# A graph layer's gather and sum: a product with zeros ahead of each product, and more chunks gathered by ScalarE

## The chip, the cores and the metric

The kernel runs on 1 core of one Trainium2 chip. The metric is the device time of one execution in microseconds (us); less is better. TensorE (PE), VectorE (DVE), ScalarE (ACT), GpSimd (POOL) and SyncE (SP) each work through their own instructions in a fixed order and wait for each other by semaphores.

## The reference, cut to what matters

```python
# x: (12500, 128) f32; src, dst: (200000,) int32, sorted by dst
h = jnp.maximum(_layernorm(x, axis=-1), 0.0)
agg = jax.ops.segment_sum(h[src], dst, num_segments=12500)
deg = jax.ops.segment_sum(jnp.ones(200000), dst, num_segments=12500)
agg = agg / jnp.maximum(deg, 1.0)[:, None]
y = jax.nn.relu(agg @ Wg + h @ Ws + bg)     # 128 -> 128
y = jnp.tanh(y @ W1 + b1)                   # 128 -> 512
y = jnp.tanh(y @ W2 + b2)                   # 512 -> 512
return x + (y @ W3 + b3)                    # 512 -> 128
```

For each of 200000 edges a row of 128 numbers is fetched and added to the row of the edge's target; the means go through a small network.

## The kernel before

**Tiling.** The edges are cut into 1563 chunks of 128, in the order of their targets. The 12500 nodes are cut into blocks of 512 columns (smaller ones at the end). As targets are sorted, a chunk's targets lie in a window of 24 columns whose place is loaded into a PE register (`place`).

**The sum.** For a chunk, `rows` holds the 128 fetched rows and `oh` a 0/1 matrix of 128 by 24 that VectorE makes by comparison (`onehot`, L495), for 8 chunks at a time. `add(c)` (L643) multiplies them on PE and adds the product into the block's sum `acc[b]` in PSUM, or into `edge[b]`, a PSUM tile of up to 280 columns for chunks that may reach into two blocks. Such a tile is first written with zeros by `cleared`. All PE work is kept in program order by the class `pe` (its line is L378 for matmuls, L381 for transposes), and in f32 a matmul is two weight loads and two matmul records in the trace.

**Four ways to fetch rows.** The layer-normed nodes lie in DRAM (`htab`) and, turned, in SBUF (`tab`, 128 features by 12544 nodes).

- `gather` (L386): one indirect DMA by POOL for a chunk, into one of `AHEAD` = 24 buffers. 1323 chunks go this way, in the list `order`, and a buffer is free again when `add` has used it.
- `row_loads` (lane 0): 128 DMAs by SyncE, one row of 512 bytes each, at an address from a register; 4 buffers.
- `column_copies` (lane 1): 128 copies by ScalarE, each of one column of `tab` at an address from a register (L442); 16 addresses are loaded at a time.
- `column_pairs` (lane 2): 64 instructions by VectorE, each of which puts two columns together (L451); 16 addresses are loaded at a time.

Chunks of the last two ways are columns, not rows: `turn` (L456) transposes them on PE into a `pm` tile and ScalarE copies them out as `turned` (L476). 80 more chunks, spread in 10 groups of 8, are fetched as raw rows of `x` at the start and normed on the way.

`SHARES` (L48) says how many chunks go to lanes 0, 1 and 2; the slots are every fourth chunk between 104 and 1540, dealt out evenly. `load_times` spreads the copies and loads of a lane over the chunks between its uses, in steps of four copies, four rows or eight pairs, so that they are issued between the other work of their engine.

**The network.** The layers of a block (`part0` to `part4`) are cut into single PE products of up to 512 columns, and one of them is put between the products of the chunks at every second chunk; ScalarE brings each result out of PSUM through its activation (`h`, L473), and the next product needs it. Three `pm` tiles are shared by these products, the turned chunks and the degree counts. From chunk 1312 on (`QUICK`) a small planner with costs per product decides how many network steps go ahead of each chunk.

**The start.** About 200 us are spent on layer norm, indices and weights; the sums begin in between, and the copies of lanes 1 and 2 after some 240 us.

Of the kernel before, what the change touches and what calls it, by code (L numbers as in the profile page):

```python
# [22 lines left out]
F32 = mybir.dt.float32  # L23
# [8 lines left out]
P = 128  # L32
# [12 lines left out]
SPREAD = 8  # L45
EVERY = 4
AT = 3
SHARES = 14, 50, 96  # L48
FROM, UNTIL = 104, 1540
SBUFS = 4  # L50
MARGIN = 18
# [14 lines left out]
PAST = 255  # L66
MAY_BE_OFF = 240
SEEN = 656
TOLD = 14
EARLY = 3  # L70

# [6 lines left out]
def windowed(ctx, tc, x, src, dst, Wg, Ws, bg, W1, b1, W2, b2, W3, b3, out, flag):  # L78
    nc = tc.nc
# [19 lines left out]
    def raw(c):  # L99
        return RAW0 <= c < RAW1 and (c - RAW0) % STEP < GRP  # L100
# [7 lines left out]
    def window(c):  # L108
        if raw(c):
            return per * (c - c % GRP) + first(W_RAW, per * GRP), W_RAW  # L110
        w = [w for c0, w in WINDOWS if c0 <= c][-1]
        return per * c + first(w), w
# [4 lines left out]
    ahead_of = P + MAY_BE_OFF  # L117
    past_end = P * (each + 1) + SEEN
    pad_dst = 2 * N // (PAST + 1) * (PAST + 1) + PAST
    assert each * N == E and pad_dst >= 2 * N - PAST and 0 < NT * P - N < P  # L120
    under, over = off + -(-ahead_of // each), off + -(-(SEEN - MAY_BE_OFF) // each)
    assert off + max(under, over) <= PAST
# [3 lines left out]
    slots = [c for c in range(AT, NCH, EVERY) if FROM <= c < UNTIL and not raw(c)]  # L126
    owed = [0.5 * n for n in SHARES] + [0.5 * (len(slots) - sum(SHARES))]
    for c in slots:
        owed = [o + n for o, n in zip(owed, [*SHARES, len(slots) - sum(SHARES)])]
        kind = max(range(4), key=lambda k: owed[k])  # L130
# [14 lines left out]
    const = ctx.enter_context(tc.tile_pool(name="const", bufs=1))  # L145
# [30 lines left out]
    for g in range(NRAW):  # L176
        t = raws.tile([P, GRP, D], F32, name=f"raw{g}")
# [7 lines left out]
    ident = const.tile([P, P], F32, name="ident")  # L185
# [27 lines left out]
    bases = const.tile([NROW, CPR], I32, name="bases")  # L213
    zeros = const.tile([P, P], BF16, name="zeros")
    nc.vector.memset(zeros, 0.0)
    begins = const.tile([1, NT], I32, name="begins")
    parity = const.tile([P, 2], F32, name="parity")
    for i in range(2):
# [153 lines left out]
    rows_t, ohs, acc = {}, {}, {}  # L372
# [10 lines left out]
    def sp_dma(*a):  # L383
        tc.keep_in_program_order(nc.sync.dma_start(*a))
# [132 lines left out]
    def seen(t):  # L517

        if t % TOLD == 0:
            u = min(t + TOLD, NT)  # L520
            loads, vs = nc.values_load_multi_w_load_instructions(
# [5 lines left out]
            told.update(enumerate(vs, t))  # L527
        w = ed.tile([P, SEEN], U8, name="nearby", bufs=4)
        at_v = bytes_at[bass.ds(told.pop(t), (P - 1) * each + SEEN)]
        sp_dma(w, bass.AP(tensor=at_v.tensor, offset=at_v.offset, ap=[[each, P], [1, SEEN]]))  # L530
        nearby[t] = w
# [48 lines left out]
    for c in range(NCH):  # L580
        lo, w = window(c)
# [21 lines left out]
    edge = {}  # L603

    def edge_span(b):
        spans = [window(c) for c in across[b]]
        return min(lo for lo, _ in spans), max(lo + w for lo, w in spans)
# [3 lines left out]
    def place(c, a0, a1):  # L611

        if raw(c):
            lo, w = window(c)
            return slice(max(lo, a0), min(lo + w, a1)), slice(max(lo, a0) - lo, min(lo + w, a1) - lo)
        if c not in places_of:
            r, q = divmod(c, CPR)
            k = next((i for i in range(q, CPR) if raw(r * CPR + i) or r * CPR + i == NCH), CPR)
            loads, vs = nc.values_load_multi_w_load_instructions(
                bases[r : r + 1, q:k], engines=[mybir.EngineType.PE], min_val=0, max_val=N - W,  # L620
                skip_runtime_bounds_check_because="brought between its ends on VectorE",
            )
            for ld in loads:
                tc.keep_in_program_order(ld)
            places_of.update(enumerate(vs, c))
        lo, w = window(c)
        most = min(lo + w, a1) - W
        at_v = places_of.pop(c).with_bounds(min_val=min(max(lo, a0), most), max_val=most)
        return bass.ds(at_v, W), slice(0, W)

    def moved(s, by):
        if isinstance(s, slice):
            return slice(s.start - by, s.stop - by)
        return bass.ds(s.start - by, W)

    def cleared(pool, name, w):
        t = pool.tile([P, BLK], F32, name=name)
        pe.matmul(
            t[:, :w], zeros, zeros[:, :1].to_broadcast([P, w]), start=True, stop=False, skip_group_check=True
        )  # L640
        return t

    def add(c):  # L643
        rows, oh = rows_t.pop(c), ohs[c // GRP][:, c % GRP]
        b = min(b for b, cs in enumerate(reach) if c in cs)
        n, m = blocks[b]
        if c in across[b]:
            e0, e1 = edge_span(b)
            if c == across[b][0]:
                edge[b] = cleared(ps_b, "edge", e1 - e0)  # L650
            to, of = place(c, e0, e1)
            pe.matmul(
                edge[b][:, moved(to, e0)], rows, oh[:, of], start=False, stop=(c == across[b][-1]), skip_group_check=True
            )
            if c == across[b][-1]:
                sums = ed.tile([P, 288], F32, name="sums", bufs=4)
                act.copy(sums[:, : e1 - e0], edge.pop(b)[:, : e1 - e0])
                edges[b] = sums
            return
        if b not in acc:  # L660
            acc[b] = cleared(ps_a, "agg", m)
        to, of = place(c, n, n + m)
        pe.matmul(
            acc[b][:, moved(to, n)], rows, oh[:, of], start=False, stop=(c == inside[b][-1]), skip_group_check=True
        )
# [216 lines left out]
    for c in range(NCH):  # L882
# [33 lines left out]
        if c >= QUICK:  # L916
# [4 lines left out]
            while soonest() and max(now, soonest()[2]) < there:  # L921
                go_on(soonest())
            now = max(now, there) + 0.27
        add(c)

        lead = LEAD if c < QUICK else 2
# [359 lines left out]
@with_exitstack  # L1286
def gnn_kernel(ctx: ExitStack, tc: tile.TileContext, *args):
    nc = tc.nc
    keep = ctx.enter_context(tc.tile_pool(name="flags", bufs=1))
    flag = keep.tile([1, 1], I32, name="flag")  # L1290
    with ExitStack() as inner:
        windowed(inner, tc, *args, flag)
    outside = nc.values_load(flag, min_val=0, max_val=P)
    with tc.If(outside > 0):
        with ExitStack() as inner:
            general(inner, tc, *args)
# [31 lines left out]
```

## Time and profile before

| | |
|---|---|
| median of 3 runs | 2167.27 us (2161.28 to 2171.19) |
| the profiled execution | 2164.96 us |
| its span, first to last instruction | 2163.2 us |
| mean granted PE clock | 0.750 |
| busy: PE, DVE, ACT, POOL | 1474.7, 1274.1, 933.4, 1335.4 us |
| gathers by POOL | 1323 of 951 ns |
| column copies by ScalarE | 6400 |
| column pairs by VectorE | 6144 |
| row loads by SyncE | 1792 |

Times are of one profiled execution. An engine's busy time does not count register loads, semaphores or the issue of DMAs. "Issue" as a cause of idle time means that the profile shows nothing the engine waited for; "remote" that the releaser could not be named. In rows of the order of time the columns are the start, the time taken, engine, line, operation, tile written and read, count, and in brackets the idle time before.

### The profile page before, as it was taken

To read this page: it belongs to the slowest core of one execution; us is meant where nothing else is said; L and a number is where in the kernel's file an instruction comes from. 1 tells how busy PE (TensorE), PEld (TensorE's weight loads), DVE (VectorE), ACT (ScalarE), POOL (GpSimd) and SP (SyncE) were. 2 spreads that over 40 slices of the span, in tenths; PEclk is the share of its full clock that TensorE was granted. 3 is DMA by queue.
4 is the path that set the end of the run, shared out by engine and by line. 5 is a ranking of instruction groups with operands and counts; after the bars stand their busy time and mean duration, and the time that the engine had idled before them with its cause. 6 is when DMAs were issued, how large, how long until landed. Compare 5 with 4: busy or idle time off the path is not lost.

```text
span 2163.2 us, 34925 instructions
## 1 busy us (share of the span) xinstructions
PE 1474.7 (68%) x5402; PEld 981.4 (45%) x5402; DVE 1274.1 (59%) x7014; ACT 933.4 (43%) x6907; POOL 1335.4 (62%) x1411
## 2 busy tenths in 40 slices
PE   0025543768687787776885876767787687798587
PEld 0024433445454454454553544545454454454457
DVE  3854365756466675665673765666576476566530
ACT  1201144545544444454544445445454454545432
POOL 7756666566666666666666566666666666666661
PEclk9999985766866766776676776777766776788589
DMA  5934221222221222222222122122222122221210
GB/s 137 243 99 124 58 51 49 52 54 58 54 58 49 61 59 55 54 61 59 52 59 57 49 59 58 51 59 60 51 57 63 47 61 66 53 61 53 56 48 22
DMA packets 132962, 139.16 MB, mean 64 GB/s; under 512 B 31655, under 2 KB 109347, under 8 KB 132536
## 3 DMA queue, kind: packets, MB, share of 16 engines
q0 software_dynamic: 44896, 92.04, 16.7%
q1 hardware_dynamic: 84558, 41.29, 7.1%
q10 hardware_dynamic: 3276, 3.51, 0.6%
q14 instruction: 181, 1.48, 0.2%
q8 instruction: 51, 0.84, 0.2%
HBM read 123.71 MB, written 13.03 MB: 63 GB/s over the span
## 4 chain that ended last, share of the span: by engine, by line
PE 37%; DVE 20%; issue 17%; another core or an unknown queue 11%; ACT 9%; DVEq 2%; DMA 1%; ACTq 1%; SPq 0%
PE pm L378 24%; DVE cols L451 12%; PE agg L378 7%; ACT cols L442 7%; PE edge L378 3%; DVEq L399 2%; ACT h L473 2%; PE pt L381 1%; DVE nearby L535 1%; ACTq L399 1%; PE pm L381 1%; DVE mT L689 1%; DVE oh L495 1%; DVE h L241 1%
## 5 line engine op out<-in xcount | busy, mean ns | idle before, releaser
L388 POOL DMA_INDIRECT rows<-htab,scol x1323 | 1257.7, 951 | 759.7 <-issue 294.0
L451 DVE SCALAR_TENSOR_TENSOR cols<-first_only,tab 128x2 f32<-128x2 f32 x6144 | 913.8, 217 | 404.8 <-issue 394.7
L378 PE MATMUL pm<-h,w 128*128 128x512 f32 (+4 forms) x1344 | 836.1, 724 | 184.1 <-ACT h L473 66.8
L442 ACT COPY cols<-tab 128x1 f32 x6400 | 713.9, 188 | 489.1 <-issue 482.3
L378 PEld LDWEIGHTS agg<-oh,rows 128*128 128x128 f32 x1914 | 420.2, 275 | 285.1 <-issue 269.9
L378 PE MATMUL agg<-oh,rows 128*128 128x24 f32 x1914 | 382.1, 314 | 38.7 <-issue 35.0
L378 PEld LDWEIGHTS pm<-h,w 128*128 128x128 f32 x1344 | 253.7, 237 | 213.7 <-ACT h L473 71.6
L378 PEld LDWEIGHTS edge<-oh,rows 128*128 128x128 f32 x732 | 138.7, 238 | 96.1 <-issue 91.1
L473 ACT ACTIVATE h<-pm,b2c 128x512 f32<-128x512 f32 (+4 forms) x112 | 70.7, 631 | 173.7 <-PE pm L378 57.7
L378 PE MATMUL edge<-oh,rows 128*128 128x24 f32 x732 | 131.3, 286 | 17.6 <-issue 14.0
L805 DVE TENSOR_TENSOR o<-pt,xb 128x512 f32<-128x512 f32 x23 | 15.9, 692 | 203.9 <-remote 83.2
L495 DVE TENSOR_TENSOR oh<-shared,dloc 128x192 f32<-128x192 f32 x186 | 64.8, 350 | 86.2 <-remote 34.1
L473 ACT ACTIVATE h<-pm,b1c 128x512 f32<-128x512 f32 (+4 forms) x112 | 70.1, 631 | 99.5 <-remote 33.6
L476 ACT COPY turned<-pm 128x128 f32<-128x128 f32 x146 | 38.2, 262 | 158.2 <-PE agg L378 60.6
L378 PE MATMUL pm<-ident,cols 128*128 128x128 f32 x192 | 57.9, 394 | 54.8 <-ACT h L473 27.3
L179 POOL DMA_INDIRECT raw<-in_x_dram,rsrc x80 | 76.8, 960 | 25.6 <-issue 24.1
L535 DVE TENSOR_SCALAR_CACHE_REDUCE nearby<-nearby,parity 128x656 uint8<-128x656 uint8 x98 | 87.0, 887 | 6.1 <-issue 6.1
L285 PE MATMUL pm<-ident,idx_f 98*128 98x98 f32 x32 | 6.2, 376 | 108.4 <-DVE idx_f L279 68.5
L378 PEld LDWEIGHTS pm<-ident,cols 128*128 128x128 f32 x192 | 40.9, 257 | 71.3 <-ACT h L473 33.8
L378 PEld LDWEIGHTS agg<-oh,turned 128*128 128x128 f32 x194 | 47.2, 270 | 55.9 <-issue 35.0
L381 PE MATMUL pt<-ident,xb 128*128 128x128 f32 x98 | 27.1, 431 | 61.0 <-issue 32.8
L381 PE MATMUL pm<-ident,degs 128*128 128x128 f32 x99 | 24.9, 374 | 62.9 <-ACT h L473 30.3
(120 smaller groups left out, 808.3 us busy)
## 6 DMA issues: line engine op xcount, KB each, us to landing
srows<-htab SPq DMA_DIRECT2D x1792, 0.5 KB
rows<-htab,scol POOLq DMA_INDIRECT x1323
nearby<-bytes_at SPq DMA_DIRECT2D x98, 82.0 KB
xb<-htab SPq DMA_DIRECT2D x24, 256.0 KB
xb<-in_x_dram SPq DMA_DIRECT2D x23, 256.0 KB
out_dram<-o SPq DMA_DIRECT2D x23, 256.0 KB
xt<-in_x_dram SPq DMA_DIRECT2D x8, 640.0 KB
htab<-h SPq DMA_DIRECT2D x8, 640.0 KB
```

The source lines that it names most:

```text
L179: nc.gpsimd.indirect_dma_start(out=t[:, j, :], out_offset=None, in_=x, in_offset=bass.IndirectOffsetOnAxis(ap=rsrc[:, g, j : j + 1], axis=0),)
L241: nc.vector.scalar_tensor_tensor(h, xt, 0.0, spread(stats[:, 1], k), op0=ALU.max, op1=ALU.mult)
L378: tc.keep_in_program_order(nc.tensor.matmul(*a, **k))
L381: tc.keep_in_program_order(nc.tensor.transpose(*a, **k))
L388: nc.gpsimd.indirect_dma_start(out=r, out_offset=None, in_=htab, in_offset=bass.IndirectOffsetOnAxis(ap=scol[:, c : c + 1], axis=0),)
L399: loads, vs = nc.values_load_multi_w_load_instructions(places[min(lane, 1)][r : r + 1, q // EVERY, p0 : p0 + LOADS[lane]], engines=[kind], ...
L442: tc.keep_in_program_order(nc.scalar.copy(to[:, t : t + 1], of))
L451: last[:] = [tc.keep_in_program_order(nc.vector.scalar_tensor_tensor(to, first_only, a, b.to_broadcast([P, 2]), op0=ALU.mult, op1=ALU.add))]
L473: tc.keep_in_program_order(nc.scalar.activation(*a, **k))
L476: tc.keep_in_program_order(nc.scalar.copy(*a))
L495: newest[:] = [nc.vector.tensor_tensor(oh[:, :k, :w], lane[:, None, :w].to_broadcast([P, k, w]), dloc[:, g * GRP : g * GRP + k][:, :, None ...
L535: done = nc.vector.tensor_scalar(w, w, parity[:, t % 2 : t % 2 + 1], None, op0=ALU.is_equal, op1=ALU.add, accum_out=found[:, t : t + 1])
```

## The change

Three constants change: lane 0 gets 22 chunks, lane 1 gets 90 and lane 2 gets 94, so that 206 chunks are fetched without POOL and 1277 by it. A tile `none` of 96 columns of zeros is set once. Ahead of each chunk's product, `kept_busy` adds a product of the unit matrix with up to 96 columns of zeros to the first columns of the same PSUM tile. It adds nothing to the sums.

```diff
-SHARES = 14, 50, 96
+SHARES = 22, 90, 94
...
+FILL = 96
...
+    none = const.tile([P, FILL], F32, name="none")
+    nc.vector.memset(none, 0.0)
...
+    def kept_busy(t, w):
+
+        w = min(w, FILL)
+        pe.matmul(t[:, :w], ident, none[:, :w], start=False, stop=False, skip_group_check=True)
+
     def add(c):
...
             if c == across[b][0]:
                 edge[b] = cleared(ps_b, "edge", e1 - e0)
+            kept_busy(edge[b], e1 - e0)
             to, of = place(c, e0, e1)
...
         if b not in acc:
             acc[b] = cleared(ps_a, "agg", m)
+        kept_busy(acc[b], m)
         to, of = place(c, n, n + m)
```

## The prediction

> **What bounds the kernel now.** I read the page's head, its chain of work that ended last and its groups, then one table for the long middle stage (400 to 2000 us), the waits in that stage, and single microseconds of the order of time.
>
> ```profile
> span 2163.2 us, 34925 instructions
> PE 1474.7 (68%) x5402; PEld 981.4 (45%) x5402; DVE 1274.1 (59%) x7014; ACT 933.4 (43%) x6907; POOL 1335.4 (62%) x1411
> ...
> PE 37%; DVE 20%; issue 17%; another core or an unknown queue 11%; ACT 9%; DVEq 2%; DMA 1%; ACTq 1%; SPq 0%
> ```
>
> No engine is full, and PE holds only 37% of the chain. The engines run coupled, each in its own fixed order, so what counts is who waits for whom.
>
> ```profile
> 400.00:2000.00 1600.00, 1219.85 (x4251) 775.62 (x4250) 998.94 (x6019) 776.72 (x6035) 997.49 (x1055) 0.71 0.22 56
> ...
> POOL rows L388 <- PE agg L378: 144.5, 133, 3.2
> POOL rows L388 <- PE edge L378: 62.5, 60, 4.7
> ...
> PE pm L378 <- ACT h L473: 71.4, 30, 8.0
> PE pm L378 <- ACT turned L476: 44.3, 15, 7.7
> PE pm L381 <- ACT h L473: 43.1, 10, 20.4
> PE pm L381 <- ACT turned L476: 27.6, 7, 11.0
> PE pm L378 <- ACT cols L442: 18.7, 8, 4.8
> ...
> ACT cols L442 <- issue: 401.0, 682, 1.9
> ACT h L473 <- issue: 22.2, 19, 4.2
> ```
>
> The first row is busy time and count in the stage for PE, PEld, DVE, ACT and POOL in turn; the others are waits in it (sum, times, longest). POOL waits for PE to give row buffers back: 144.5 and 62.5 us. PE is busy 1220 of 1600 us and waits for ScalarE: the five rows make 205 us. So the pace of the stage is PE's stream with ScalarE's answers in it, and the gathers follow. ScalarE is busy 777 us and loses another 423 us to "issue" (401.0 + 22.2), idle that nothing else explains. What it has free is 1600 - 777 - 423 = 400 us.
>
> **ScalarE: 40 more chunks.** Each is 128 one-column copies, so 40 x 128 = 5120 more on top of the 6400 of the group below.
>
> ```profile
> L442 ACT COPY cols<-tab 128x1 f32 x6400 | 713.9, 188 | 489.1 <-issue 482.3
> ...
> 400.00:2000.00 1600.00, 629.72 (x5675) 0.71 0.22 56
> ...
> 1564.01 2.42 ACT L442 COPY cols<-tab 128x1 f32 x24 [0.42 <-issue]
> 1593.80 1.58 ACT L442 COPY cols<-tab 128x1 f32 x16 [0.41 <-issue]
> ...
> 1139.56 0.19 ACT L442 COPY cols<-tab 128x1 f32 x1 [0.52 <-issue]
> 1139.96 0.95 POOL L388 DMA_INDIRECT rows<-htab,scol  x1 [0.30 <-DMA rows<-htab,scol]
> 1140.26 0.19 ACT L442 COPY cols<-tab 128x1 f32 x1 [0.51 <-issue]
> 1141.21 0.95 POOL L388 DMA_INDIRECT rows<-htab,scol  x1 [0.30 <-issue]
> ```
>
> The second row is the stage again, for the copies alone: 5675 of the 6400 lie in it, so the stage gets 0.8 x 5675 = 4540 more. One copy has three prices. At best copies follow each other as in the row of 24: 2.42 / 24 = 0.101 us. With the idle before such runs (the load of 16 addresses), the two runs together give (2.42 + 0.42 + 1.58 + 0.41) / 40 = 0.121 us. Over the whole execution, busy and idle, it is (713.9 + 489.1) / 6400 = 0.188 us. The dear part is in stretches like the one at 1139.56, where a copy starts every 0.70 us (1140.26 - 1139.56) while gathers leave POOL every 1.25 us without a pause (1141.21 - 1139.96). I take 0.121, the price of undisturbed runs, since I expect fewer such stretches when POOL waits more, and keep 0.101 and 0.188 as ends. The chunks also have to be turned on PE and brought out of PSUM, for 40 more of ScalarE's and 2 fewer of VectorE's:
>
> ```profile
> L476 ACT COPY turned<-pm 128x128 f32<-128x128 f32 x146 | 38.2, 262 | 158.2 <-PE agg L378 60.6 <-remote 54.5 <-PE edge L378 19.9
> L381 PE MATMUL pm<-ident,cols 128*128 128x128 f32 x50 | 19.0, 379 | 47.0 <-ACT turned L476 13.7 <-ACT h L473 12.8 <-issue 10.2
> ```
>
> That is 38 x 0.262 x 0.8 = 8 us more on ScalarE in the stage, and 40 x 0.379 = 15 us on PE in all, within the bounds of the fill below. ScalarE's extra work in the stage is 4540 x 0.121 + 8 = 557 us. It has 400 us free, so 157 us stick out even if all its waiting goes. Ends: 4540 x 0.101 + 8 = 467, which is 67 us over; 4540 x 0.188 + 8 = 862, which is 462 us over. Some waiting for PE will stay, some issue idle will go; I let these cancel. Behind the copies in ScalarE's order stand the layers' activations (h) and the turned chunks, and PE waits for just these, so an overfull ScalarE lands on PE and through it on everything.
>
> [...]
>
> **PE: a product ahead of each product.** Every one of the 1563 chunks gets a product of `ident` (128 columns of weights) with up to 96 columns of zeros, f32, so two weight loads and two matmuls each.
>
> ```profile
> L378 PE MATMUL pm<-h,w 128*128 128x512 f32 x1104 | 791.4, 809 | 175.4 <-ACT h L473 60.6 <-issue 40.0 <-remote 39.2
> L378 PE MATMUL agg<-oh,rows 128*128 128x24 f32 x1914 | 382.1, 314 | 38.7 <-issue 35.0 <-DVE cols L451 1.8 <-DMA rows<-htab,scol 0.9
> L378 PE MATMUL edge<-oh,rows 128*128 128x24 f32 x732 | 131.3, 286 | 17.6 <-issue 14.0 <-remote 3.4 <-DVE mT L687 0.2
> ...
> 1128.21 1.10 PE L378 MATMUL pm<-h,w 128*128 128x512 f32 x2
> 1129.15 0.52 PE L378 MATMUL edge<-oh,rows 128*128 128x24 f32 x4
> 1129.51 1.10 PE L378 MATMUL pm<-h,w 128*128 128x512 f32 x2
> ...
> 1137.40 0.63 PE L381 MATMUL pt<-ident,h 128*128 128x128 f32 x4
> ...
> 1561.88 1.74 PE L378 MATMUL agg<-oh,rows 128*128 128x24 f32 x8
> 1563.45 2.05 PE L378 MATMUL pm<-h,w 128*128 128x512 f32 x2
> 1570.28 0.77 PE L378 MATMUL pm<-ident,cols 128*128 128x128 f32 x2
> ```
>
> PE runs at two speeds: the same pair of 512 columns takes 1.10 us at 1128.21 and 2.05 us at 1563.45. At the fast one a fill of two matmuls lies between 2 x 0.09 = 0.18 us (four of 24 columns from 1129.15 to 1129.51) and 2 x 0.157 = 0.31 us (0.63 / 4, 128 columns); I take 0.285, near the wider shape. At the slow one it lies between 2 x 0.22 = 0.44 us (1.74 / 8) and 0.77 us (the pair at 1570.28); I take 0.55.
>
> In the stage are 1563 x 1055 / 1323 = 1246 fills (the share by the gathers of the table above and of the group below): 355 us at the fast speed, 685 at the slow one. Against it stands what a PE always fast would save there: the pairs of 512 columns cost 791.4 / 552 = 1.434 us of busy time each, against 0.94 (1128.21 to 1129.15), so 0.494 x 552 x 0.8 = 217 us; the chunks' matmuls cost (382.1 + 131.3) / 2646 = 0.194 us, against 0.09, so 0.104 x 3126 x 0.8 = 259 us (3126 being 1563 x 2). With the fast speed throughout, 476 - 355 = 121 us are saved; with today's mix nothing is saved and some 355 to 685 us are added, of which idle can take part. I expect most windows to become fast, not all, as PE will still stand waiting for ScalarE, with no fill issued meanwhile: a fill stands in PE's own order behind the wait. So I put PE's net at nothing, with ends -121 and the rival's below.
>
> **POOL, VectorE, SyncE.** 206 chunks leave the gathers, not 160: 46 fewer.
>
> ```profile
> L388 POOL DMA_INDIRECT rows<-htab,scol x1323 | 1257.7, 951 | 759.7 <-issue 294.0 <-PE agg L378 168.8 <-remote 154.0
> L451 DVE SCALAR_TENSOR_TENSOR cols<-first_only,tab 128x2 f32<-128x2 f32 x6144 | 913.8, 217 | 404.8 <-issue 394.7 <-DVE shared L234 0.2
> ...
> srows<-htab SPq DMA_DIRECT2D x1792, 0.5 KB
> ...
> 1131.37 22.23 SPq L384 DMA_DIRECT2D srows<-htab  x20
> ...
> 1157.81 7.75 SPq L384 DMA_DIRECT2D srows<-htab  x24
> ```
>
> 46 x 1.25 = 58 us less on POOL, hidden, since POOL waits for PE; if PE stopped making it wait, they would count in full. VectorE loses 2 x 64 x 913.8 / 6144 = 19 us, hidden as well. SyncE goes from 1792 to 22 x 128 = 2816 one-row transfers at 0.32 us (7.75 / 24) to 1.11 us (22.23 / 20): 901 to 3126 us. No row of the waits shows PE waiting for such a row, and I put it at 0. That cover is thin: at the middle of the two prices, 0.72, it is 2028 us, more than the stage's 1600 and its borders hold, so the high end would add some 200 us or more beside the main term. Queued behind these transfers on SyncE are the blocks' loads and the stores.
>
> The sum: the profiled execution took 2164.96 us (1.8 outside its span), 2.3 under the median of 2167.27. 2165 + 157 + 2 = 2324 us.
>
> **The rivals.**
>
> *The clock holds and PE speeds up (faster).* The fills keep PE fast throughout, its 121 us come off, and PE's quicker answers leave ScalarE room: 2167 - 121 = 2046 us. For it: the granted clock is 0.71 in the stage (the column after POOL in its first row), and 2.05 against 1.10 is a large prize. Against it: ScalarE at its cheapest is still 67 us over, so the 423 us of issue idle must shrink by at least 188 us. It decides if ScalarE's idle before copies falls from 0.188 - 0.112 = 0.076 us a copy to near 0.02.
> [...]
>
> *The fills run at the slow speed (slower still).* The idle windows stay, the speeds keep their mix, and a fill costs the mean of 0.285 and 0.55, 0.42 us: 1246 x 0.42 = 523 us on PE. Of PE's 380 us idle in the stage the 205 of ScalarE stay and 175 are used: 2167 + 348 = 2515 us. For it: PE is busy 76% of the stage at that mix already. [...]
>
> *Nothing to be seen.* ScalarE's overhang is made up by the faster products: 67 - 121 + some waiting, about 2167 us. It takes the cheap end twice.
>
> **How the numbers follow.** Main case 0.58 (2324, own range 2234 to 2629), the faster rival 0.26, the slow fills 0.11, nothing 0.05. A measurement of this kernel tells about 0.5% from no change. Faster by over that: the faster rival and a little of the third, 0.27; within it 0.04; slower 0.69. The range leaves out about half of the faster rival's spread (2010 to 2150) below and the ends of the main case and the slow fills above: 2060 to 2530 us.
>
> **What would show it.** Right: ScalarE's busy time near 933 + 5120 x 0.11, about 1500 us, its free time in the middle stage near nothing, PE's waits for ACT (h, turned, cols) well over 205 us, POOL's waits for PE longer. PE's clock up, pairs of 512 columns mostly at 1.10 us, and fills at 0.18 to 0.31 us each. Wrong: copies at 0.10 us with little issue idle and PE's waits for ScalarE no longer than now; then the stage is set by the gathers at 1.25 us. Slow fills would show as pairs at 2.05 us as often as now and PE busy over 90% of the stage.

## The result, and the profile after

The kernel after the change takes 2337.09 us in the median of 4 runs (2329.81 to 2352.51), against 2168.3 for the kernel before: 1.079 times as long (95% interval 1.073 to 1.085). The forecast was 2324 us. The experiments further down ran on three chips on which the kernel before takes 1782 to 1783 us, so a time there is compared with the kernel before on the same chip. The chip of this measurement isn't on record; below, "the result's chip" stands for wherever the kernel before takes 2168 us. Executions more than 1.5% above the fastest of their kernel are left out of the ratios: one of four in e5 and three of four in e4, the profiled one of e4 among them.

The page of the kernel after, its head and its chain:

```profile
span 2337.8 us, 48549 instructions
PE 1893.8 (81%) x8560; PEld 1431.5 (61%) x8560; DVE 1235.4 (53%) x6887; ACT 1429.3 (61%) x12065; POOL 1291.8 (55%) x1365
...
PE 55%; ACT 17%; issue 10%; DVE 7%; another core or an unknown queue 7%; ACTq 1%; DMA 1%; DVEq 1%; SPq 0%
PE pm L381 28%; PE agg L381 20%; ACT cols L445 15%; PE edge L381 6%; DVE cols L454 3%; ACT h L476 2%; PE pt L384 1%; ACTq L402 1%; PE pm L384 1%; DVEq L402 1%; DVE agg L230 1%; DVE h L244 1%; DVE agg L237 1%; DMA xt<-in_x_dram 0%
```

The row of the chain by lines in the kernel before:

```profile
PE pm L378 24%; DVE cols L451 12%; PE agg L378 7%; ACT cols L442 7%; PE edge L378 3%; DVEq L399 2%; ACT h L473 2%; PE pt L381 1%; DVE nearby L535 1%; ACTq L399 1%; PE pm L381 1%; DVE mT L689 1%; DVE oh L495 1%; DVE h L241 1%
```

PE holds 55% of the chain, not 37%, and the products into the sums (agg, edge) 26%, not 10%. ScalarE's share rose too, from 9% to 17%, most of it copies (7% to 15%). PE is 419 us busier (1893.8 - 1474.7) and 245 us less idle ((2163.2 - 1474.7) - (2337.8 - 1893.8)); the difference, 174 us, is what the span grew. Over 1563 fills, 419 us are 0.27 us each. The stage 400 to 2000 us, with the waits in it (sum, times, longest):

```profile
400.00:2000.00 1600.00, 1398.14 (x6113) 1027.52 (x6113) 876.32 (x5333) 1094.66 (x9537) 863.25 (x913) 0.73 0.18 50
...
PE pm L381 <- DVE rd L599: 57.5, 10, 10.3
PE pm L381 <- ACT turned L479: 26.7, 7, 8.2
PE pm L381 <- ACT h L476: 21.3, 8, 5.8
PE pm L381 <- ACT cols L445: 17.3, 4, 9.9
PE pm L384 <- ACT h L476: 9.5, 5, 2.7
...
POOL rows L391 <- PE agg L381: 372.9, 248, 8.7
POOL rows L391 <- PE edge L381: 131.3, 94, 8.0
...
ACT cols L445 <- issue: 317.9, 621, 1.2
ACT h L476 <- issue: 42.3, 33, 4.9
...
L445 ACT COPY cols<-tab 128x1 f32 x11520 | 1217.0, 188 | 418.1 <-issue 400.8
```

PE is busy 87% of the stage (it was 76%). Its waits for ScalarE fell from 205 to 75 us (the four ACT rows), and POOL's waits for PE rose from 207 to 504 us: 913 gathers pass in the stage where 1055 did. So the waits name PE as the engine that holds the others up, and not ScalarE, though ScalarE is nearly full as well: 1600 - 1095 - 360 leaves it 145 us, where it had 400. PE's longest wait is now one for VectorE's copies of the degree counts (rd), 57.5 us; why these come late isn't shown. The granted clock is 0.73, where it was 0.71.

What a fill costs stands in the order of time, first at PE's fast speed, then at the slow one (start, time taken):

```profile
1130.76 1.10 PE L381 MATMUL pm<-h,w 128*128 128x512 f32 x2
1131.70 0.36 PE L381 MATMUL edge<-none,ident 128*128 128x96 f32 x2
1131.89 0.33 PE L381 MATMUL edge<-oh,rows 128*128 128x24 f32 x2
1132.06 0.44 PE L381 MATMUL edge<-none,ident 128*128 128x96 f32 x2
1132.34 0.33 PE L381 MATMUL edge<-oh,rows 128*128 128x24 f32 x2
1132.51 1.10 PE L381 MATMUL pm<-h,w 128*128 128x512 f32 x2
...
1012.77 2.06 PE L381 MATMUL pm<-h,w 128*128 128x512 f32 x2
1014.62 0.58 PE L381 MATMUL agg<-none,ident 128*128 128x96 f32 x2
1014.99 0.51 PE L381 MATMUL agg<-oh,turned 128*128 128x24 f32 x2
1015.33 0.72 PE L381 MATMUL agg<-none,ident 128*128 128x96 f32 x2
1015.85 0.51 PE L381 MATMUL agg<-oh,rows 128*128 128x24 f32 x2
1016.18 2.05 PE L381 MATMUL pm<-h,w 128*128 128x512 f32 x2
```

A round of two chunks and a product of 512 columns takes 1.75 us at the fast speed; before it was 1.30 (1128.21 to 1129.51 in the trace of before), so a fill costs 0.225 us. At the slow speed two chunks with fills take as long as four without did: 3.41 us here (1012.77 to 1016.18), and 3.41 us for four chunks and a product before, from this row to the one at 1563.45 that the prediction shows:

```profile
1560.04 2.05 PE L378 MATMUL pm<-h,w 128*128 128x512 f32 x2
```

So a fill costs there what a chunk costs. Four equal shares of 3.41 - 1.85 (the product, 1012.77 to 1014.62) make 0.39 us.

### The profile page after: what moved, and what is told of

Same layout as the page of the kernel before. It is cut to its first block, busy times and chain, and to the rows that moved or that the text cites. A ratio compares the mean times of both kernels' runs of the same rounds, so it can differ in the third digit from the quotient of the medians.

```text
span 2337.8 us, 48549 instructions
## 1 busy us (share of the span) xinstructions
PE 1893.8 (81%) x8560; PEld 1431.5 (61%) x8560; DVE 1235.4 (53%) x6887; ACT 1429.3 (61%) x12065; POOL 1291.8 (55%) x1365
## 3 DMA queue, kind: packets, MB, share of 16 engines
q8 instruction: 76, 1.25, 0.2%
## 4 chain that ended last, share of the span: by engine, by line
PE 55%; ACT 17%; issue 10%; DVE 7%; another core or an unknown queue 7%; ACTq 1%; DMA 1%; DVEq 1%; SPq 0%
PE pm L381 28%; PE agg L381 20%; ACT cols L445 15%; PE edge L381 6%; DVE cols L454 3%; ACT h L476 2%; PE pt L384 1%; ACTq L402 1%; PE pm L384 1%; DVEq L402 1%; DVE agg L230 1%; DVE h L244 1%; DVE agg L237 1%; DMA xt<-in_x_dram 0%
## 5 line engine op out<-in xcount | busy, mean ns | idle before, releaser
L391 POOL DMA_INDIRECT rows<-htab,scol x1277 | 1211.9, 949 | 976.1 <-PE agg L381 455.3
L445 ACT COPY cols<-tab 128x1 f32 x11520 | 1217.0, 188 | 418.1 <-issue 400.8
L454 DVE SCALAR_TENSOR_TENSOR cols<-first_only,tab 128x2 f32<-128x2 f32 x6016 | 869.3, 218 | 277.6 <-issue 271.7
L381 PE MATMUL pm<-h,w 128*128 128x512 f32 (+4 forms) x1344 | 814.4, 705 | 105.0 <-ACT h L476 28.1
L381 PEld LDWEIGHTS agg<-none,ident 128*128 128x128 f32 x2236 | 518.7, 263 | 309.9 <-issue 307.8
L381 PE MATMUL agg<-none,ident 128*128 128x96 f32 x2236 | 593.6, 357 | 12.1 <-issue 11.9
L381 PEld LDWEIGHTS agg<-oh,rows 128*128 128x128 f32 x1846 | 398.5, 266 | 10.2 <-issue 10.0
L381 PE MATMUL agg<-oh,rows 128*128 128x24 f32 x1846 | 393.1, 295 | 10.9 <-issue 10.5
L381 PEld LDWEIGHTS edge<-none,ident 128*128 128x128 f32 x890 | 181.7, 232 | 114.5 <-issue 114.0
L381 PE MATMUL edge<-none,ident 128*128 128x96 f32 (+1 forms) x890 | 209.7, 322 | 5.3 <-issue 5.3
```

What stands on the lines that cost most here:

```text
L381: tc.keep_in_program_order(nc.tensor.matmul(*a, **k))
L391: nc.gpsimd.indirect_dma_start(out=r, out_offset=None, in_=htab, in_offset=bass.IndirectOffsetOnAxis(ap=scol[:, c : c + 1], axis=0),)
L445: tc.keep_in_program_order(nc.scalar.copy(to[:, t : t + 1], of))
L454: last[:] = [tc.keep_in_program_order(nc.vector.scalar_tensor_tensor(to, first_only, a, b.to_broadcast([P, 2]), op0=ALU.mult, op1=ALU.add))]
```

## The experiments

All times are medians where nothing else is said, with the ratio to the kernel before on the same chip. The theory after the result is called PE: the fills cost PE's time and PE is the bound. The rival, called ScalarE, is the prediction's own: the added copies cost it. Edits are shown against the kernel after for e1, e3, e4, e7, e11 and e12, against the kernel before for e2 and its repeats, and against e2 for e8 and e9. e1 to e4 ran on one chip, e5 to e8 on a second, e9 to e12 on a third.

**The fills alone** (e1, and again on another chip as e11):

```diff
-SHARES = 22, 90, 94
+SHARES = 14, 50, 96
```

> The fills alone, with the old shares 14, 50, 96. Theory PE (the fills themselves cost the time: PE 419 us busier, partly in place of idle): about 2340 us, 2280 to 2400, as the new shares then give nothing or a little. Rival ScalarE (the 5120 more copies cost the time, as the prediction had it): about 2170 us, at most 2210, PE's waits for ScalarE as before (205 us in the stage 400 to 2000 us).

> The fills alone once more, for the same case: where the kernel before takes about 2168 us theory PE says about 2340 us (ratio 1.05 to 1.10), rival ScalarE at most 2210. Where before takes 1782 us: about 1810 us, as before.

Measured: 1813.06 us, ratio 1.013 (1.008 to 1.019), and 1806.84 us, ratio 1.010 (1.006 to 1.014). Slower, as theory PE has the sign, but by far less than 8%. The times of e1's expectation were made for a chip on which before takes 2168 us. Taken as ratios, the outcome lies with the rival (at most 2210, 1.02) and not with theory PE (1.05 to 1.11); of e11's, the 1810 us for this kind of chip came out. The stage 400 to 1600 us of e1:

```profile
400.00:1600.00 1200.00, 1157.86 (x6118) 851.17 (x6136) 861.40 (x5314) 654.84 (x5433) 907.62 (x960) 0.90 0.27 69
```

PE is busy 96% of it, at a clock of 0.90, and still 960 gathers pass: one in 1.25 us, POOL's own pace. PE just keeps up.

**The shares alone** (e2, and twice again on two other chips as e6 and e10), no fills:

```diff
-SHARES = 14, 50, 96
+SHARES = 22, 90, 94
```

> The new shares 22, 90, 94 alone, no fills. Theory PE: at or below 2167 us, about 2110, for 46 gathers fewer (58 us) come off a POOL that has less to wait for. Rival ScalarE: about 2320 us (2230 to 2400), ScalarE's free time in the middle stage near nothing and PE waiting for it well over 205 us.

> The new shares alone, as before, to split the change on the same chip as the whole of it. Theory PE: faster than the kernel before on any chip, ratio 0.97 where no copies are held up; where they are (before at 2168 us) between 0.97 and 1.02. Rival ScalarE, for a chip with held-up copies: 1.05 to 1.08, as ScalarE's copies cost 0.188 us there and not 0.10.

> The new shares alone once more, for the case that the chip of this call is one where the kernel before takes about 2168 us: there, theory PE says 0.97 to 1.02 of before, rival ScalarE 1.05 to 1.08. Where before takes 1782 us: 1732 us, as twice before.

Measured: 1732.36, 1733.38 and 1734.66 us, ratios 0.972 (0.969 to 0.975), 0.972 and 0.973: faster by 50 us, close to 46 gathers at 1.25 us (58). The groups of e2 for ScalarE's copies, and its stage:

```profile
L442 ACT COPY cols<-tab 128x1 f32 x11520 | 1150.3, 188 | 38.6 <-issue 26.5 <-ACT sums L476 0.9 <-ACT h L473 0.8
...
400.00:1600.00 1200.00, 1063.10 (x4012) 680.10 (x4032) 900.35 (x5553) 1078.33 (x9916) 907.23 (x961) 0.79 0.27 70
```

A copy costs (1150.3 + 38.6) / 11520 = 0.103 us here, with hardly any issue idle. ScalarE is busy 90% and yet POOL goes at its own pace, 961 gathers. For the shares alone the rival falls on these three chips. On the chip of the result a copy cost 0.188 us before and (1217.0 + 418.1) / 11520 = 0.142 after; none of these runs had such a chip, so the shares alone weren't seen there.

**The whole change on the second kind of chip** (e5, no edit):

> The whole change once more, beside kernels of one part each. On the chip of the first four runs, where the kernel before takes 1783 us and no copy stands 0.7 us apart from the next, theory PE says: the fill of 96 columns is dense enough to keep PE fast, PE is the bound at about 97% busy, 1790 to 1840 us (ratio 1.00 to 1.03). Rival (PE falls into the slow speed as with 24 columns): 2200 to 2300 us. On a chip where the kernel before takes about 2168 us: 2337 us.

Measured: 1856.35 us, ratio 1.041 (1.034 to 1.048), a little over what was expected; e6 ran beside it on the same chip. The four kernels make a square: the shares alone 0.972, the fills alone 1.010 to 1.013, both 1.041. So the fills cost 1% on the old shares and 7% on the new ones (1.041 / 0.972), and the shares gain 2.8% without fills and cost some 3% with them (1.041 / 1.013). The loss is not that of one part; it is mostly that of the two together. The stage, and PE's largest wait in it:

```profile
400.00:1600.00 1200.00, 1136.89 (x5944) 847.78 (x5961) 841.89 (x5163) 1008.62 (x9239) 852.46 (x903) 0.87 0.25 66
...
PE pm L381 <- DVE rd L599: 45.0, 15, 5.9
```

PE is busy 95% and 903 gathers pass, not 961: what the shares freed on POOL, PE cannot take. With the old shares (e1) no wait for rd is among PE's; here it takes 45 us of the stage, as it does in e2 (45.0), where PE has time for it. That is about what the shares cost on top of the fills (1856 us against 1813), but no run tests whether it is the cause, and what delays rd isn't shown.

**A cheaper fill** (e3): zeros in bf16 by zeros in bf16, one weight load and one matmul.

```diff
-        pe.matmul(t[:, :w], ident, none[:, :w], start=False, stop=False, skip_group_check=True)
+        pe.matmul(t[:, :w], zeros, zeros[:, :w], start=False, stop=False, skip_group_check=True)
```

> The whole change, but with the fill in bf16 (zeros by zeros, 128 columns of weights, 96 moving), so one weight load and one matmul in place of two dearer ones. Theory PE: the loss shrinks with the fill's price, to a third or so: 2190 to 2250 us. Rival ScalarE: the loss does not hang on the fill's price: 2310 to 2340 us. If a fill is good for the clock, this one keeps it as well, and the pairs of 512 columns at 1.10 us stay at 65% or more.

Measured: 1750.06 us, ratio 0.982 (0.979 to 0.985): 18 us above the shares alone, where the f32 fill costs about 120 (e5 over e6). As a ratio it lies below both forecasts (1.01 to 1.04 and 1.07 to 1.08). The loss hangs on the fill's price, as theory PE has it, and this fill loses no clock: 0.83 in the stage, against 0.79 in e2.

```profile
400.00:1600.00 1200.00, 1088.03 (x5193) 681.06 (x5210) 896.46 (x5513) 1077.38 (x9904) 907.33 (x960) 0.83 0.27 70
```

**Fewer columns in the fill** (e4), and **at every second chunk only** (e12, which has both edits):

```diff
-FILL = 96
+FILL = 24
```

```diff
-            kept_busy(edge[b], e1 - e0)
+            if c % 2:
+                kept_busy(edge[b], e1 - e0)
...
-        kept_busy(acc[b], m)
+        if c % 2:
+            kept_busy(acc[b], m)
```

> The whole change, with FILL = 24 in place of 96: the weight loads stay, a quarter of the columns. Theory PE: a fill then costs what a product of a chunk costs, 0.18 us at the fast speed in place of 0.22 and about the same in the slow one per weight load: 2270 to 2320 us. Rival ScalarE: 2320 to 2340 us. If the time falls to 2200 or below, it is the columns that cost, not the weight loads.

Measured: 2227.95 us in the fastest of four runs (to 2279.25) where before takes 1782.89 (1779.46 to 1789.79): 25% more, by a fill that was to be cheaper. Both theories missed it, as ratios (1.05 to 1.08). The profiled execution took 2278.79 us, at the same mean clock of 0.74 as the fastest. The group of the large products in e4, its stage, a round in the order of time, a rest of PE with what follows, and 80 us of the stage:

```profile
L381 PE MATMUL pm<-h,w 128*128 128x512 f32 x1104 | 881.6, 894 | 18.9 <-DVE rd L599 13.2 <-ACT h L476 4.4 <-ACT turned L479 0.9
...
400.00:1600.00 1200.00, 1170.25 (x4310) 853.05 (x4324) 612.94 (x3730) 743.14 (x6731) 610.67 (x648) 0.63 0.18 47
...
1001.81 1.10 PE L381 MATMUL pm<-h,w 128*128 128x512 f32 x2
1002.75 0.30 PE L381 MATMUL edge<-none,ident 128*128 128x24 f32 x2
1002.89 0.38 PE L381 MATMUL edge<-oh,rows 128*128 128x24 f32 x2
1003.12 0.38 PE L381 MATMUL edge<-none,ident 128*128 128x24 f32 x2
1003.34 0.38 PE L381 MATMUL edge<-oh,rows 128*128 128x24 f32 x2
1003.56 1.10 PE L381 MATMUL pm<-h,w 128*128 128x512 f32 x2
...
1023.29 0.49 PE L381 MATMUL pm<-ident,cols 128*128 128x128 f32 x2 [3.19 <-DVE rd L599]
...
1024.54 1.80 PE L381 MATMUL pm<-h,w 128*128 128x512 f32 x2
...
1030.00:1110.00 80.00, 80.00 (x249) 57.28 (x248) 35.93 (x212) 49.99 (x464) 40.57 (x43) 0.50 0.16 41
```

At the fast speed the round takes 1.75 us with 24 columns (1001.81 to 1003.56), just as with 96 (1130.76 to 1132.51 above), so the 72 further columns add nothing to it. That the weight loads make the price is a reading of these two rounds; no run shows it by itself. What differs from e5 is the clock: PE is busy 98% of the stage and gets 0.63, where e5 has 0.87; the pair of large products takes 894 ns a matmul in the mean, against 695 in e5 and 771 in e2.

Following the pairs of 512 columns through the stage (1.10 us fast, 2.05 us slow), one finds 7 falls to the slow speed in e4, and 5 of them come within 3 us of the end of a rest of 3 to 6 us, as at 1024.54. In e5 there are 16 falls, each within 6 us of the end of a rest of over 1 us. So in these two runs the slow speed begins mostly after a rest, with 24 columns as with 96. What differs is how long it stays: 129 us in the mean in e4, 19 us in e5. From 1030 to 1110 us in e4 PE is busy all the time and the clock stays at 0.50, so being busy did not end it there. A guess at what may end it is how much of PE's time streams columns. Counting the columns of both records of each matmul, a round of the fast speed has 1024 for the product, 96 for the two chunks and the fills' own: without fills 1120 in 1.30 us, 862 a microsecond; with 24 columns 1216 in 1.75, 695; with 96 columns 1504 in 1.75, 859. From these densities came the expectation of e12:

> As with FILL = 24, but the fill stands only ahead of every second chunk. [...] Theory density (the share of streaming cycles in PE's stream sets how long the fast speed is held): between e4 and the shares alone, 1850 to 2050 us where the kernel before takes 1782, with 0.55 to 0.7 of the pairs of 512 columns fast. Rival (any fill costs its weight loads and no more): 1732 + 782 x 0.2 = at most 1790 us.

Measured: 2061.62 us, ratio 1.156 (1.150 to 1.162), 12 us outside the range given, with a clock of 0.64 in the stage and 891 ns a matmul.

```profile
400.00:1600.00 1200.00, 1144.40 (x4143) 792.88 (x4156) 719.38 (x4387) 861.58 (x7846) 710.38 (x755) 0.64 0.21 55
```

The rival falls, also with its sum put right (1732 + 782 x 0.2 is 1888 us, not 1790): such fills cost 327 us over e10 on the same chip. The clock is hardly better than in e4 though the stream is denser (1168 columns in a round of an estimated 1.53 us, 1.305 without fills and 0.2225 for one: 763 a microsecond).

**More columns in the fill** (e7):

```diff
-FILL = 96
+FILL = 288
```

> The whole change with up to 288 columns of zeros in place of 96. If columns cost at 2 cycles each at the fast speed, a fill grows from 0.22 to about 0.48 us: 1563 x 0.26 = 406 us more on a PE that is the bound, with the fast speed held all the time: 2150 to 2250 us where the kernel before takes 1783. Rival (the weight loads are the price, the columns run beside them): 1800 to 1900 us.

Measured: 1997.44 us, ratio 1.120 (1.118 to 1.122), between the two.

```profile
L381 PE MATMUL pm<-h,w 128*128 128x512 f32 x1104 | 611.9, 638 | 21.7 <-DVE rd L599 16.8 <-ACT h L476 4.7 <-issue 0.2
...
400.00:1600.00 1200.00, 1170.61 (x5385) 840.89 (x5400) 765.32 (x4676) 919.99 (x8354) 772.50 (x819) 0.98 0.23 60
...
1000.22 1.11 PE L381 MATMUL pm<-h,w 128*128 128x512 f32 x2
1001.16 0.65 PE L381 MATMUL agg<-none,ident 128*128 128x288 f32 x2
1001.65 0.30 PE L381 MATMUL agg<-oh,rows 128*128 128x24 f32 x2
1001.79 0.73 PE L381 MATMUL agg<-none,ident 128*128 128x288 f32 x2
1002.36 0.30 PE L381 MATMUL agg<-oh,rows 128*128 128x24 f32 x2
1002.50 1.11 PE L381 MATMUL pm<-h,w 128*128 128x512 f32 x2
```

The fill's price was forecast right: the round is 2.28 us, so a fill is (2.28 - 1.30) / 2 = 0.49 us. The cycles a column that the forecast counts with are shown by no run; against the round of 1.75 us with 96 columns, 384 more columns a fill, in its two matmuls, cost (2.28 - 1.75) / 2 = 0.265 us. The forecast had the fast speed too, but left out what it takes off all the other products: the clock is 0.98 in the stage at 996 columns a microsecond, against 0.87 with 96 columns, and a large product's matmul takes 638 ns, where e5's takes 695.

The density of the stream, counted in rounds of the fast speed, beside the falls to the slow speed in the stage, how long it stays in the mean, and the clock:

| run | columns a us | falls | slow for | clock |
|---|---|---|---|---|
| e4, 24 columns | 695 | 7 | 129 us | 0.63 |
| e12, 24 at every second chunk | 763 | 11 | 73 us | 0.64 |
| e1, 96 columns, old shares | 859 | 9 | 24 us | 0.90 |
| e5, 96 columns | 859 | 16 | 19 us | 0.87 |
| e2, no fills | 862 | 32 | 15 us | 0.79 |
| e7, 288 columns | 996 | 5 | 8 us | 0.98 |

In these six runs the slow speed ends sooner where the stream is denser, most plainly between 695 and 859. How often it begins is another matter: most often without fills, where PE is idle 11% of the stage. Between e4, e5 and e7 the columns are the only edit. That it is the columns streamed which the chip counts isn't shown beyond these rows.

**Other shares without fills**, to beat e2: more for VectorE (e8) and more for SyncE (e9).

```diff
-SHARES = 22, 90, 94
+SHARES = 24, 92, 112
```

> No fills, and shares 24, 92, 112: 22 gathers fewer than with 22, 90, 94. Where POOL is the bound (gathers at 1.25 us without a pause): 1732 - 22 x 1.25 = 1705 us, the fastest of all. Rival (ScalarE and VectorE are full by now): 1730 us or more. Where the kernel before takes 2168 us: no better than with 22, 90, 94.

```diff
-SHARES = 22, 90, 94
+SHARES = 32, 88, 96
```

> No fills, shares 32, 88, 96: 10 gathers fewer than with 22, 90, 94, and the lane that is used more is SyncE's. POOL as the bound: 1732 - 10 x 1.25 = 1720 us. Rival (SyncE cannot keep up with 4096 rows, or VectorE is full): 1735 us or more.

Measured: 1785.02 us, ratio 1.001 (1.000 to 1.002), and 2032.99 us, ratio 1.140 (1.137 to 1.143). Both came out on the rival's side. The chain of e8, then that of e9 with its largest wait and a stretch of SyncE's queue:

```profile
DVE 45%; PE 15%; issue 13%; ACT 11%; POOL 6%; DVEq 5%; DMA 4%; ACTq 1%; POOLq 0%
...
SPq 47%; issue 16%; PE 13%; DVE 10%; DMA 8%; ACT 3%; POOL 1%; DVEq 1%; ACTq 0%; POOLq 0%
...
DVE nearby L535 <- DMA nearby<-bytes_at: 297.7, 47, 15.2
...
1003.95 21.68 SPq L384 DMA_DIRECT2D srows<-htab  x52
```

In e8 VectorE is full: busy 1000 us of the 1200 from 400 to 1600, and 189 more idle before its column pairs with no cause named (issue). In e9 SyncE is: 21.68 / 52 = 0.42 us a row, so 4096 rows take 1708 us, and the loads for the degree counts (nearby) queue behind them. The shares 22, 90, 94 without fills are the fastest version that was run, ahead of the kernel before on three chips and of the kernel after on the one where both ran.

## Why the prediction was right or wrong

**The sign and the size came out (2324 forecast, 2337 measured), but, as far as the runs show, not for the reason given.** The sum had 157 us from ScalarE and nothing from PE. What is shown is that on three chips the shares alone make the kernel faster (0.972), and that on one of them the fills on top cost 7%. On the result's chip the parts weren't run alone; its trace points the same way: PE busier by 419 us, its waits for ScalarE down from 205 to 75 us, POOL's for PE up from 207 to 504. Against it stands ScalarE's larger share of the chain there (17%); but e2 has 23% in a kernel that got faster. Nor are the new shares free once the fills are there: they cost some 3% (e5 against e1), though PE's waits for ScalarE are 10 us of e5's stage. The agreement of 2324 with 2337 is luck.

**The step that failed: "ScalarE: 40 more chunks".** The copies were taken at 0.121 us; on the result's chip they cost 0.142 and elsewhere 0.103. The sum has 557 us of new work against 400 us free. In the 1600 us of the stage ScalarE became 318 us busier (777 to 1095), lost 63 us less to issue and still had 145 us free: with PE slower, less of its work falls into the stage, and it did not run out of time. That an overfull ScalarE lands on PE was the wrong link. Of the signs named beforehand, ScalarE's busy time came near (1429 us for about 1500), while PE's waits for it went the other way, and that one decides.

**The step that failed with it: "PE's net at nothing".** The fill's two prices were taken at 0.285 and 0.55 us and are 0.225 and 0.39: the narrow 24-column shape was the nearer neighbour, since 96 columns cost no more than 24 (both rounds 1.75 us). The slow price even lies below the range of 0.44 to 0.77, because 1.74 us is the time to the end of the last of eight matmuls; start to start, 1561.88 to 1563.45, it is 1.57, 0.39 a pair. The error was in setting the dearer chunks off against a faster clock. That most windows would become fast was an estimate of the author; the clock of the stage went from 0.71 to 0.73 only, and PE's work grew by more than its idle could take. The prediction's own sign for slow fills, pairs at 2.05 us as often as before, nearly held (a large product's matmul took 809 ns in the mean and takes 791).

**The rivals.** "The fills run at the slow speed" came nearest to what happened: the mix of speeds kept, PE as the bound. It gave 2515 us as it charged 0.42 a fill and kept the 205 us of ScalarE's waits, of which 130 vanished. The faster rival fails on the clock: with 96 columns it is 0.87 in the stage (e5) and 0.79 without fills (e2) on the second kind of chip, 0.73 and 0.71 on the first, and the price stays. Nor does a busier PE always get a better mix: in e4 it is busy 98% of the stage at a clock of 0.63, where e2 has 89% and 0.79.

**POOL, VectorE, SyncE** stood right as far as they were tested: the 58 us of POOL are hidden while PE holds it up, and come out (50 us) when it doesn't. SyncE's cover, called thin, is gone at 4096 rows; at 2816 no wait in the rows shows it.

**The clock.** The prediction expects slow windows where PE stands waiting, and fast ones where fills keep it busy. The traces agree on the first half: 5 of e4's 7 falls come within 3 us of the end of a rest of 3 to 6 us, and each of e5's 16 within 6 us of the end of a rest of over 1 us. On the second e4 does not: with PE busy all 80 us from 1030 to 1110 the clock stays at 0.50. In that stretch a stream of weight loads and few columns did not win the fast speed back.

**The copies.** A copy takes 188 ns, on the result's chip as in e2. In e2 the next one follows after 0.103 us in the mean, so they overlap there.

**Open:** the split between the two parts on the result's chip, why copies in some stretches there start only every 0.70 us, and why the new shares delay rd.

## What to carry to other kernels

Price an instruction added to a busy engine's stream by the round it stands in, start to start, at each speed: here a fill of 96 columns in f32 costs 0.225 or 0.39 us, and at the fast speed one of 24 columns costs the same. A filler pays only if it is cheaper than what a faster clock gives back: here neither the f32 fill was (some 120 us lost, e5 over e6) nor the bf16 one (18 us, e3 over e2). With one of 24 columns the slow speed lasted 129 us in the mean (e4). Run two changes made at once in all four combinations: the shares here gain 2.8% alone, and with the fills beside them they cost.

## What the runs showed of the hardware that was not expected

- The same kernel took 2168 us where the result was measured and 1782 to 1783 on three chips later, a fifth less. In the first trace there are stretches in which ScalarE copies once in 0.70 us while gathers leave POOL without a pause; in e2 POOL gathers without a pause and a copy takes 0.103 us.
- A fill of 24 columns costs PE the same round as one of 96 (1.75 us), and yet makes the kernel some 370 us slower (2227.95 and 1856.35 us, on two chips where before takes the same): the slow speed, once begun, lasts 129 us in the mean and not 19.
